# A first row map for two expert slots, and two reorderings in the local attention

## The chip, the cores and the metric

The kernel is written for one Trainium2 chip and runs on one of its cores. A core has five engines with queues of their own: TensorE (PE; its weight loads are shown apart as PEld), VectorE (DVE), ScalarE (ACT), GpSimd (POOL) and SyncE (SP), which here mostly issues DMAs. The metric is the device time of one execution in microseconds (us), the median over several runs. The profile is of one further execution, with a span of its own.

## The reference, cut to what matters

Four blocks work on `x`, four images of 512 tokens with 256 features each (all fp32):

```python
x = x + linear_attention(mixture_of_experts(x, cond))
x = x + local_layers(cond_attention(x, cond))      # two layers

# mixture of experts: 8 experts, each token goes to its two best
gate_w = softmax(rms_norm(x) @ wg_W + wg_b + cond @ gg_W + gg_b)
topk_w, topk_i = top_k(gate_w, 2)
h1 = relu(x @ W1[e] + b1[e]);  h2 = relu(h1 @ W2[e] + b2[e]);  out_e = h2 @ W3[e] + b3[e]
out = sum over the two experts of topk_w * out_e

# each local layer: windowed attention (8 heads of 64, windows of 128), then a gated FFN
q, k, v = split(shift_token(x) @ wqkv)
q, k = rotary_xpos(l2norm(q) * qs, l2norm(k) * ksc)
x = x + softmax(mask(8 * q @ k.T)) @ v @ wo
x = x + (a * gelu(g)) @ w2 + b2                     # a, g from layernorm(shift_token(x)) @ w1 + b1
```

## The kernel before

**Routing and experts.** Tokens are sorted by expert into slots of one or two groups of 128 rows; each slot runs one expert's three matrices. VectorE computes for every token and both of its choices a position, split into a high part (row group and half) and a low part (0 to 63): the tile `hl` (L1438). The *row map* says which token stands in which row. It is made with matmuls: for each of 16 token tiles and both choices, a one-hot of the low part (`ol`, L1456, 64 columns, multiplied by the token number) is the stationary operand and a one-hot of the high part (`oh`, L1461, 80 columns) the moving one; 32 products add up in `pmap`. `half_map` (L1473) copies the sum, two more matmuls fold the halves (`pmap2`), and `rowtok` (L1478) holds the token number of each row, for all 40 row groups, `goal` the row of the output table `ys`. `busy(4)` (L1494) runs four matmuls that no one reads, in program order behind the map.

`loads` (L1508) reads a slot's expert number from `eid` and issues its three weight DMAs on SP's queue (L1511, L1513, L1517); the weight buffers are two deep. `fetch` (L1529) gathers a slot's rows on POOL's queue with `rowtok` as index. `turn_tokens` transposes them on TensorE (`pxb`) and ScalarE copies them out. The loop over the slots runs layer 1 (`ph`), issues the next loads and gathers, the previous slot's last layer (`po`), transposes the next slot's rows, and runs layer 2. Slot 0 has one row group, slot 1 two.

**Order.** Instructions are scheduled by a planner, except those that are pinned: TensorE's in a `PE.in_order()` block, and what goes through `pinned` or `keep_in_program_order`. Each engine then works off its own queue in a fixed order and stops at the first instruction whose inputs are missing.

**Local attention.** `front` (L634) is a generator for one image: two transposed halves (`pdt`), then for four token tiles `t` and for q and k (`s`) a projection `pdq`, its squares on ScalarE (L658), their sums `ss` on VectorE (L659), a product with a table over the whole width (`t1`, L661), two products over half the width (`t2`, L665), and a sum of the two on POOL (L668, `qr`). After all eight: the root on ScalarE (L672), the maximum and reciprocal on VectorE (L673, L674), three value projections, and for each tile the scaling of q (L686) and transposes `pqt` into `qT` and `kT`.

The attention runs in steps `k`, four to an image (`c` is a pair of heads): `scores` (`pds`, exponentials L720, masks L723 and L726), `values` of the step before (`pn`, added into `oT`, L745), and on odd steps `sums`, the denominators of two pairs (`pz`). `sums` goes through DRAM to turn a row into a column and back: `z` to `sums_`, to `rd`, reciprocal (L770), to `rows_` (L772), and two broadcasts into `zb` (L775), all on SP's queue, then two multiplies on `oT` (L778). `beside(b)` is the filler work of the next image's `front` and the previous image's `tail` (`pdy`, the output product that reads `oT`); `spend(n)` takes `n` steps of it. `first_two` (L902) opens each layer with the front of image 0 and two steps of the front of image 1: in layer 0 with nothing beside it, in layer 1 beside the feed-forward work of layer 0.

## Time and profile before

| | us |
|---|---|
| median of 3 runs | 1338.26 (1338.1 to 1339.82) |
| profiled execution, its own time | 1341.16 |
| its span | 1339.4 |
| TensorE busy in it | 1273.7 |
| VectorE busy | 685.6 |
| ScalarE busy | 581.6 |
| POOL busy | 292.8 |

The mean granted clock of TensorE in that execution is 0.983 of full speed. The experts run to about 300 us, the linear and conditioned attention to about 694 us, and the two local layers from there to the end.

Rows of a group or of the timeline read: start or engine, line of the kernel, operation, output tile <- input tiles, partitions x elements, and in brackets how long the engine sat idle before it and what ended that. A matmul in fp32 leaves two records per instruction of the kernel, a transpose one.

### The profile page before, as it was taken

The page shows a single profiled execution, that of the slowest core. Times are in us where ns is not written, and L with a number is a line of the kernel's source. Part 1 is how long each engine was busy: PE and PEld are TensorE (multiplying, and loading weights), DVE is VectorE, ACT ScalarE, POOL GpSimd, SP SyncE. Part 2 cuts the span into 40 slices and gives each one's busy share as a digit, 9 for nine tenths or more (in the row PEclk, how much of TensorE's full clock was granted, in tenths as well). Part 3 has the DMA queues.
Part 4 walks back from the last instruction along what each step waited for, and adds up shares of the span by engine and source line. Part 5 has one row for each costly group of instructions (what it writes and reads, how often), then busy time and mean ns, then how long its engine had stood idle before and what let it go on. Part 6 is the DMA issues. An engine that isn't in the chain of part 4 may idle for free.

```text
span 1339.4 us, 23071 instructions
## 1 busy us (share of the span) xinstructions
PE 1273.7 (95%) x9214; PEld 812.9 (61%) x9214; DVE 685.6 (51%) x1464; ACT 581.6 (43%) x1158; POOL 292.8 (22%) x321
## 2 busy tenths in 40 slices
PE   4899999998999999999999999999999998999998
PEld 3788899964566634444344655766556556667654
DVE  6221243425777734241247798654362877864421
ACT  3221233226655365656644646561222655464111
POOL 1322356420000201010103334210030333422010
PEclk7999999998999999999999999999999999999999
DMA  3565666523000000000220001311001011012000
GB/s 95 212 232 199 233 235 226 183 101 101 0 1 1 1 1 1 0 1 1 91 71 1 18 18 27 104 34 25 24 0 44 25 30 31 18 43 57 17 20 23
DMA packets 41856, 85.29 MB, mean 64 GB/s; under 512 B 9409, under 2 KB 25673, under 8 KB 39433
## 3 DMA queue, kind: packets, MB, share of 16 engines
q1 hardware_dynamic: 36600, 73.02, 16.9%
q0 software_dynamic: 3504, 9.46, 2.1%
q8 instruction: 77, 1.26, 0.4%
q10 hardware_dynamic: 1632, 1.21, 0.3%
q14 instruction: 43, 0.34, 0.1%
HBM read 74.76 MB, written 6.82 MB: 61 GB/s over the span
## 4 chain that ended last, share of the span: by engine, by line
PE 76%; DVE 10%; DMA 6%; ACT 4%; issue 3%; POOL 0%; SPq 0%; DVEq 0%; POOLq 0%
PE ph L82 11%; PE pdq L82 7%; PE pfy L82 6%; PE sc L82 6%; PE pua L82 5%; PE pug L82 5%; PE pv L82 5%; PE pdy L82 4%; PE po L82 3%; PE pn L82 3%; DMA ys<-ob,goal 2%; PE pds L82 2%; PE pqk L82 2%; PE pz L82 1%; PE pqt L86 1%
## 5 line engine op out<-in xcount | busy, mean ns | idle before, releaser
L82 PE MATMUL pdq<-wqkv,yT 128*128 128x512 f32 x384 | 172.4, 599 | 2.5 <-DVE t L665 2.2
L424 ACT ACTIVATE cex<-sc 128x512 f32<-128x512 f32 x256 | 132.0, 605 | 85.8 <-PE sc L82 84.8
L82 PEld LDWEIGHTS pdq<-wqkv,yT 128*128 128x128 f32 x384 | 71.5, 191 | 85.0 <-issue 76.7
L82 PE MATMUL ph<-h,w 128*128 128x256 f32 (+2 forms) x576 | 121.4, 369 | 0.3 <-ACT h L1635 0.3
L668 POOL TENSOR_TENSOR qr<-t,t 128x512 f32<-128x512 f32 x64 | 81.3, 1271 | 138.2 <-DVE t L665 138.2
L82 PEld LDWEIGHTS ph<-h,w 128*128 128x128 f32 x576 | 101.5, 191 | 15.7 <-ACT h L1635 0.5
L1500 DVE TENSOR_SCALAR h<-ph,w 128x256 f32<-128x256 f32 (+2 forms) x52 | 23.0, 462 | 122.1 <-PE ph L82 101.6
L82 PE MATMUL sc<-qm,kT 32*128 32x512 f32 x512 | 83.0, 647 | 0.0
L720 ACT ACTIVATE p<-pds,ss 128x192 f32<-128x192 f32 (+1 forms) x256 | 79.8, 425 | 2.1 <-PE pds L82 0.8
L82 PE MATMUL pua<-hT,w 128*128 128x512 f32 x160 | 75.3, 593 | 1.1 <-DVE z L745 1.1
L82 PE MATMUL pug<-hT,w 128*128 128x512 f32 x160 | 76.1, 598 | 0.0
L658 ACT ACTIVATE sq<-pdq 128x512 f32<-128x512 f32 x64 | 38.5, 601 | 84.0 <-POOL qr L668 46.6
L753 POOL TENSOR_TENSOR p<-p 128x192 f32<-128x192 f32 x64 | 42.1, 678 | 137.7 <-PE pn L82 134.9
L835 ACT ACTIVATE gl<-pug,cols 128x512 f32<-128x512 f32 x40 | 27.3, 687 | 93.3 <-PE pug L82 90.4
L82 PE MATMUL pv<-cex,v 128*32 128x512 f32 x512 | 61.7, 598 | 2.7 <-DVE vw L378 2.7
L82 PE MATMUL pfy<-w,uA 128*128 128x256 f32 x256 | 61.4, 383 | 0.0
L82 PE MATMUL po<-w,h 128*128 128x256 f32 x264 | 60.1, 380 | 0.0
L723 DVE TENSOR_TENSOR p<-p,lmask 128x384 f32<-128x384 f32 x64 | 47.1, 736 | 23.2 <-ACT p L720 21.8
L82 PE MATMUL pdy<-wo,oT 128*128 128x256 f32 x256 | 58.7, 383 | 0.0
L1498 ACT ACTIVATE h<-ph,w 128x256 f32<-128x256 f32 (+2 forms) x52 | 22.4, 455 | 82.5 <-PE ph L82 78.7
L82 PE MATMUL pn<-p,v 64*64 64x128 f32 (+1 forms) x1792 | 50.4, 254 | 7.6 <-DVE p L726 3.7
L836 DVE SCALAR_TENSOR_TENSOR uA<-pua,cols,gl 128x512 f32<-128x512 f32 x32 | 23.8, 749 | 65.6 <-PE pua L82 56.1
(361 smaller groups left out, 2325.1 us busy)
## 6 DMA issues: line engine op xcount, KB each, us to landing
w<-in_moe_w_dram SPq DMA_DIRECT2D x18, 1024.0 KB, 8.3
w<-in_moe_w_dram SPq DMA_DIRECT2D x18, 516.0 KB, 3.8
w<-in_moe_w_dram SPq DMA_DIRECT2D x14, 640.0 KB, 4.3
zb<-rows SPq DMA_DIRECT2D x32, 256.0 KB, 4.2
g<-ys SPq DMA_DIRECT2D x6, 512.0 KB, 6.4
wqkv<-in_f_wqkv_dram SPq DMA_DIRECT2D x2, 1536.0 KB
w<-in_f_w_dram SPq DMA_DIRECT2D x2, 1408.0 KB
w<-in_moe_w_dram SPq DMA_DIRECT2D x4, 512.0 KB
```

Source lines behind the costliest of these rows:

```text
L82: cls._queue(nc.tensor.matmul(*args, **kw))
L86: cls._queue(nc.tensor.transpose(*args, **kw))
L424: nc.scalar.activation(ex[:, i, :], pss[2 * j + i], AF.Exp, scale=CHD**-0.5)
L658: nc.scalar.activation(sq, p3, AF.Square)
L668: nc.gpsimd.tensor_tensor(qr_t[:, s], t1, t2, ALU.add)
L720: nc.scalar.activation(p[:, j * 192 : j * 192 + n], pss[j // 2][r][:, j % 2 * 192 : j % 2 * 192 + n], AF.Exp, scale=d.ss[:, j, 1, 2 * c + ...
L723: nc.vector.tensor_tensor(edges, edges, lmask[:, :128].rearrange("p (s q) -> p s q", q=64).unsqueeze(1).to_broadcast([128, 3, 2, 64]), ALU ...
L753: nc.gpsimd.tensor_tensor(p[:, 1:, 0:64], p[:, 1:, 0:64], p[:, : NT - 1, 128:], ALU.add)
L835: nc.scalar.activation(gl, pg, AF.Gelu, bias=col("bg", l * (NU + 1) + i))
L836: nc.vector.scalar_tensor_tensor(f.u[i // 4][:, i % 4, :], pa, col("ba", l * (NU + 1) + i), gl, ALU.add, ALU.mult)
L1498: pinned(nc.scalar.activation(dst, src, AF.Relu, bias=bias))
L1500: pinned(nc.vector.tensor_scalar(dst, src, bias, 0.0, ALU.add, ALU.max))
```

## The change

*Routing.* Ahead of the full map a first map is made for the three row groups of slots 0 and 1 alone: one-hots of the high part over six columns (`oh0`, which here carries the token numbers), raw one-hots of the low part (`ols`), 32 products of six columns, a copy, two fold matmuls and a `rowtok` of three columns. The gathers of slots 0 and 1 use it. The full map then uses the same `ols`, multiplied by the token numbers in place; three of its four groups of products stand ahead of slot 0's transposes on TensorE, the fourth behind them, and its fold and `rowtok` come after slot 0's first layer. Slot 1's and later weights read the expert number from `eids`, a copy of `eid` that is made behind the full one-hots and depends on the first map. `busy(4)` becomes `busy(7)` ahead of the map, and `busy(2)` and `busy(1)` among the full products. Slot 1's transposes move in between slot 0's second-layer matmuls.

*Local attention.* In `front`, the root, the maximum, the reciprocal and the scaling of the first tile's q move ahead of the last two half products. In layer 0 image 0's first `pqt` bank gets five matmuls of the identity ahead of its transposes. `sums` becomes a generator with two stops: the matmuls, `z` and the first two DMAs come where they were, the reciprocal and the broadcasts at the end of that step, and the multiplies a step later.

```diff
@@ -650,6 +650,11 @@
             d.ss = ss = lp.tile([128, NT, 2, DH], F32, tag="ss", name="ss")
             qr = []
+            def unit(t):
+                tc.keep_in_program_order(nc.vector.tensor_tensor(
+                    qr[t][:, 0], qr[t][:, 0], ss[:, t, 0].unsqueeze(2).to_broadcast([128, DH, DHD]), ALU.mult))
             for t in range(NT):
                 qr_t = lp.tile([128, 2, DH, DHD], F32, tag="qr", name="qr", bufs=4)
                 for s in range(2):
@@ -660,18 +665,22 @@
                     t1 = lp.tile([128, DH, DHD], F32, tag="t1", name="t1")
                     nc.vector.tensor_tensor(
                         t1, p3, w.tab[:, 2 * s, t, :].unsqueeze(1).to_broadcast([128, DH, DHD]), ALU.mult)
+                    if t == NT - 1 and s == 1:
+                        nc.scalar.activation(ss, ss, AF.Sqrt)
+                        tc.keep_in_program_order(nc.vector.tensor_scalar_max(ss, ss, 1e-12))
+                        tc.keep_in_program_order(nc.vector.reciprocal(ss, ss))
+                        unit(0)
                     t2 = lp.tile([128, DH, DHD], F32, tag="tmp", name="t2", bufs=3)
                     for d0, d1 in ((0, 32), (32, 0)):
-                        nc.vector.tensor_tensor(
+                        ins = nc.vector.tensor_tensor(
                             t2[:, :, d0 : d0 + 32], p3[:, :, d1 : d1 + 32],
                             w.tab[:, 2 * s + 1, t, d0 : d0 + 32].unsqueeze(1).to_broadcast([128, DH, 32]), ALU.mult)
+                        if t == NT - 1 and s == 1:
+                            tc.keep_in_program_order(ins)
                     nc.gpsimd.tensor_tensor(qr_t[:, s], t1, t2, ALU.add)
                     yield
                 qr.append(qr_t)
-            nc.scalar.activation(ss, ss, AF.Sqrt)
-            nc.vector.tensor_scalar_max(ss, ss, 1e-12)
-            nc.vector.reciprocal(ss, ss)
             d.v = lp.tile([128, NT, DH, DHD], F32, tag="v", name="v")
             d.kT = lp.tile([128, 4, S], F32, tag="kT", name="kT")
             d.qT = lp.tile([128, 4, S], F32, tag="qT", name="qT")
@@ -683,10 +692,15 @@
                 value(t)
                 yield
             for t in range(NT):
-                nc.vector.tensor_tensor(
-                    qr[t][:, 0], qr[t][:, 0], ss[:, t, 0].unsqueeze(2).to_broadcast([128, DH, DHD]), ALU.mult)
+                if t > 0:
+                    nc.vector.tensor_tensor(
+                        qr[t][:, 0], qr[t][:, 0], ss[:, t, 0].unsqueeze(2).to_broadcast([128, DH, DHD]), ALU.mult)
                 for s, dst in enumerate((d.qT, d.kT)):
                     pt = mmt("pqt")
+                    if t + s == 0 and awake:
+                        with PE.in_order():
+                            for _ in range(awake):
+                                PE.matmul(pt[:, 0:128], ident, ident, start=True, stop=True)
                     for c in range(4):
                         PE.transpose(pt[:, c * 128 : (c + 1) * 128],
                                      qr[t][:, s, 2 * c : 2 * c + 2, :].rearrange("p h d -> p (h d)"), ident)
@@ -763,10 +777,11 @@
                 PE.matmul(later[:, :, 64:], ones32[64:], p[64:, :, 0:64], start=True, stop=True)
                 PE.matmul(later[:, 1:, 0:64], ones32[64:], p[64:, : NT - 1, 64:128], start=True, stop=True)
             together(z, pz)
-            rd = rdenl[:, (l * B + b) * 2 + c // 2, :]
             sums_ = dr.tile([4, S], F32, tag="sums", name="sums")
             nc.sync.dma_start(sums_, z[0:128:32, :])
+            rd = rdenl[:, (l * B + b) * 2 + c // 2, :]
             nc.sync.dma_start(rd, sums_.rearrange("h q -> (h q)").rearrange("(p n) -> p n", p=128))
+            yield
             nc.vector.reciprocal(rd, rd)
             rows_ = dr.tile([4, S], F32, tag="rows", name="rows")
             nc.sync.dma_start(rows_.rearrange("h q -> (h q)").rearrange("(p n) -> p n", p=128), rd)
@@ -774,6 +789,7 @@
             for r in range(2):
                 nc.sync.dma_start(zb[64 * r : 64 * r + 64],
                                   rows_.rearrange("(c r) q -> r c q", r=2)[r].partition_broadcast(64))
+            yield
             for i in range(2):
                 nc.vector.tensor_tensor(d.oT[c - 1 + i], d.oT[c - 1 + i], zb[:, i, :], ALU.mult)
@@ -946,11 +962,13 @@
                     for _ in range(n):
                         next(fill, None)
+                old = iter(())
                 for k in range(4 * B + 2):
                     b, c = divmod(k, 4)
                     if k > 1 and k % 2:
                         b0, c0 = divmod(k - 2, 4)
-                        sums(l, b0, ds[b0], c0)
+                        young = sums(l, b0, ds[b0], c0)
+                        next(young)
                     if c == 0 and b < B:
                         run(fill)
                         fill = beside(b)
@@ -959,7 +977,13 @@
                         values(ds[b0], c0)
                     if b < B:
                         scores(ds[b], c)
+                    if k % 2 == 0:
+                        run(old)
                     spend(6 if b < B - 1 else 3)
+                    if k > 1 and k % 2:
+                        old = young
+                        next(old)
+                run(old)
                 spend(2)
                 for _ in tail(wa, B - 1, ds[B - 1]):
                     next(ff)
...
@@ -1360,6 +1384,14 @@
             pcnt = mmt("pcnt")
             PE.matmul(pcnt[:, :NE], tot, mtiles[:, 128:], start=True, stop=True)
             PE.matmul(ppos[:, :128], tot, mtiles[:, :128], start=False, stop=True)
+            def busy(n):
+                with PE.in_order():
+                    ps = mmt("pbusy")
+                    for _ in range(n):
+                        PE.matmul(ps, ident, xres[0].rearrange("p t h -> p (t h)")[:, :512], start=True, stop=True)
+            busy(7)
             E2 = [128, NE, 3 * NE]
             over = xp.tile(E2, F32, tag="over", name="over")
             nc.vector.tensor_tensor(over, pcnt[:, :NE].unsqueeze(2).to_broadcast(E2),
@@ -1448,50 +1481,98 @@
+            def one_hot(out, of, iota):
+                shape = list(of.shape) + [iota.shape[1]]
+                for _ in of.shape[1:]:
+                    iota = iota.unsqueeze(1)
+                tc.keep_in_program_order(nc.vector.tensor_tensor(
+                    out, of.unsqueeze(len(of.shape)).to_broadcast(shape), iota.to_broadcast(shape), ALU.is_equal))
+            first = [2 * NPAIR + SLOTS[0][0], 2 * SLOTS[1][0], 2 * SLOTS[1][0] + 1]
+            oh0 = y[2].rearrange("p t h -> p (t h)")[:, : 12 * B * NT].rearrange("p (k i n) -> p k i n", k=2, n=6)
+            for at, r, n in ((0, first[0], 2), (2, first[1], 4)):
+                one_hot(oh0[:, :, :, at : at + n], hl[:, 0], miota[:, 2 * r : 2 * r + n])
+            tokens = mtok.rearrange("p (k i) -> p k i", k=2)
+            pinned(nc.vector.tensor_tensor(
+                oh0, oh0, tokens.unsqueeze(3).to_broadcast([128, 2, B * NT, 6]), ALU.mult))
+            ols = [y[k].rearrange("p t h -> p (t h)").rearrange("p (i n) -> p i n", n=64) for k in (1, 3)]
+            for i0 in (0, B * NT // 2):
+                for k in range(2):
+                    one_hot(ols[k][:, i0 : i0 + B * NT // 2], hl[:, 1, k, i0 : i0 + B * NT // 2], miota[:, :64])
+            def map_products(pmap, n, onehot, k, tiles):
+                for i in tiles:
+                    PE.matmul(pmap[64 * k : 64 * k + 64, : 2 * n], ols[k][:, i, :], onehot(k, i),
+                              start=(i == 0), stop=(i == B * NT - 1))
+            def map_copied(pmap, n):
+                half_map = xp.tile([128, n, 2], F32, tag=f"hmap{n}", name="hmap")
+                pinned(nc.vector.tensor_copy(half_map, pmap[:, : 2 * n].rearrange("p (r q) -> p r q", q=2)))
+                return half_map
+            def map_rows(half_map, n):
+                pmap2 = acct("pmap2")
+                for q in range(2):
+                    PE.matmul(pmap2[64 * q : 64 * q + 64, :n], mfold, half_map[:, :, q], start=True, stop=True)
+                rowtok = xp.tile([128, n], I32, tag=f"rowtok{n}", name="rowtok")
+                pinned(nc.vector.tensor_scalar(rowtok, pmap2[:, :n], -1.0, 0.0, ALU.add, ALU.max))
+                pinned(nc.vector.tensor_single_scalar(rowtok, rowtok, B * S - 1, op=ALU.bitwise_and))
+                return pmap2, rowtok
...
+            with PE.in_order():
+                pmap = acct("pmap")
+                for i in range(B * NT):
+                    for k in range(2):
+                        map_products(pmap, 3, lambda k, i: oh0[:, k, i, :], k, [i])
+                early_rows = map_rows(map_copied(pmap, 3), 3)[1]
+            xbs = [hp.tile([128, 2, H], F32, tag="xb", name="xb", bufs=3) for j in range(2)]
+            gather(xbs[0][:, 0, :], early_rows, 0)
+            for i in range(2):
+                gather(xbs[1][:, i, :], early_rows, 1 + i)
+            eids = xp.tile([128, 1], I32, tag="eids", name="eids")
             pmap = acct("pmap")
...
+            ohs = []
+            def full_onehots(g):
+                tiles = slice(4 * g, 4 * g + 4)
+                oh = hp.tile([128, 2, 4, NHI], F32, tag=f"h{1 + g // 2}", name="oh")
+                one_hot(oh, hl[:, 0, :, tiles], miota)
+                for i in range(4 * g, 4 * g + 4):
+                    pinned(nc.scalar.mul(ols[0][:, i, :], ols[0][:, i, :], mtok[:, i : i + 1]))
+                pinned(nc.vector.tensor_tensor(
+                    ols[1][:, tiles], ols[1][:, tiles], tokens[:, 1, tiles].unsqueeze(2).to_broadcast([128, 4, 64]),
+                    ALU.mult))
+                ohs.append(oh)
+            def full_products(g):
                 with PE.in_order():
+                    for i in range(4 * g, 4 * g + 4):
+                        for k in range(2):
+                            map_products(pmap, NROWT, lambda k, i: ohs[i // 4][:, k, i % 4, :], k, [i])
+            for g in range(4):
+                full_onehots(g)
+            pinned(nc.vector.scalar_tensor_tensor(eids, early_rows[:, 0:1], 0.0, eid, ALU.min, ALU.max))
+            busy(2)
+            for g in range(3):
+                full_products(g)
+                if g == 0:
+                    busy(1)
+            def full_rows():
+                pmap2, rowtok = map_rows(full_map, NROWT)
...
+                return rowtok, goal
...
-                e = nc.sync.value_load(eid[j : j + 1, 0:1], min_val=0, max_val=NE - 1)
+                e = nc.sync.value_load((eids if j else eid)[j : j + 1, 0:1], min_val=0, max_val=NE - 1)
...
@@ -1571,6 +1650,8 @@
                         m = m2 * k + i
                         mm(ps[:, i * n : (i + 1) * n],
                            [(w[:, c, m * 128 : (m + 1) * 128], src[:, c, 0:n]) for c in range(w.shape[1])])
+                        if between is not None and m == 2:
+                            between()
                     if d.n == 2:
                         turn[0] ^= 1
                     for i in range(k):
@@ -1707,10 +1788,12 @@
             btail = y[3][:, 0]
             htail = y[2].rearrange("p t h -> p (t h)")[:, 512:].rearrange("p (w c n) -> p w c n", w=NWIDE, c=4)
             loads(0, ds[0])
-            fetch(0, ds[0])
-            fetch(1, ds[1])
+            ds[0].xb, ds[1].xb = xbs
             with PE.in_order():
                 turn_tokens(ds[0])
+                full_products(3)
+            with PE.in_order():
+                full_map = map_copied(pmap, NROWT)
             last_wide = max(j for j, d in enumerate(ds) if d.wide)
             often, rare = ds[:-NRARE], range(len(ds) - NRARE, len(ds))
             for j, d in enumerate(often):
@@ -1728,6 +1811,8 @@
                         h1 = layer_few(d, d.xbT, d.t1, "h1", w1, d.s1, 0)
                     else:
                         h1 = layer(d, d.xbT, "h1", w1, 0)
+                    if j == 0:
+                        rowtok, goal = full_rows()
                     if j + 1 < len(often):
                         loads(j + 1, after)
                         for name in list(later)[: (j > 1) + (j > 8)]:
...
@@ -1756,9 +1839,9 @@
                     if 9 < j < 10 + B:
                         pinned(nc.gpsimd.tensor_tensor(
                             xres[j - 10], xres[j - 10], row("bo").unsqueeze(1).to_broadcast([128, NT, H]), ALU.add))
-                    if j + 1 < len(often):
+                    if 0 < j < len(often) - 1:
                         turn_tokens(after)
-                    d.h2 = layer(d, h1, "h2", d.w2, 4)
+                    d.h2 = layer(d, h1, "h2", d.w2, 4, None if j else lambda: turn_tokens(after))
                     if d.wide:
                         pinned(nc.scalar.copy(htail[:, d.at], d.h2[:, :, 256:]))
             last(len(often) - 1, often[-1])
```

Not shown: `first_two` passes the number of filler matmuls to `front` (five in layer 0, none in layer 1), and `gather` replaces the written-out gathers of the other slots.

## The prediction

> **What bounds the kernel now.** I read the busy shares first, then the chain of work that ended last in the two places that the diff touches, then the waits of TensorE and the DMAs behind them. TensorE bounds the whole:
>
> ```profile
> PE 1273.7 (95%) x9214; PEld 812.9 (61%) x9214; DVE 685.6 (51%) x1464; ACT 581.6 (43%) x1158; POOL 292.8 (22%) x321
> ```
>
> So only a stretch in which TensorE waits, or runs at a low clock, can give time back. The first is the routing. The chain there (start, length, what):
>
> ```profile
> 30.27 0.21 DVE hl L1438
> 30.50 0.69 DVE ol L1456
> ...
> 37.10 1.02 PE pmap L82 x16
> ...
> 39.51 5.26 DMA xb<-in_x_dram,rowtok
> 44.82 0.45 PE pxb L86 x2
> ...
> 45.71 3.58 PE ph L82 x16
> 49.29 0.44 PE pxb L86 x4
> 49.75 7.80 PE ph L82 x48
> ```
>
> From `hl` at 30.5 the map of all 40 row groups is built, the first gather leaves at 39.51 and takes 5.26, and the first expert starts at 45.71. From there to 257 us the chain is TensorE almost without a break, so what is won before 45.71 stays won. The busy time by stretch, whose columns after the five engines are granted clock, DMA share and GB/s:
>
> ```profile
> 30.00:35.00 5.00, 2.82 (x32) 2.64 (x32) 4.93 (x11) 2.55 (x10) 0.00 (x0) 0.50 0.83 281
> 35.00:40.00 5.00, 3.90 (x43) 2.55 (x41) 3.07 (x10) 1.70 (x7) 0.49 (x1) 0.97 1.01 415
> 40.00:45.00 5.00, 2.57 (x8) 0.95 (x6) 0.00 (x0) 0.00 (x0) 3.78 (x5) 1.00 0.74 282
> 45.00:50.00 5.00, 4.52 (x24) 4.04 (x23) 0.27 (x1) 0.74 (x2) 1.53 (x2) 0.66 0.27 79
> ```
>
> Two things: the gather competes with the weights of slots 0 and 1 (DMA share 1.01), and the clock falls to half as the first expert starts (0.66 over that stretch), so its 16 records take 3.58 us.
>
> The second place is the local attention. TensorE's waits in layer 0 (total, times, longest):
>
> ```profile
> PE pqt L86 <- DVE qr L686: 5.8, 4, 2.5
> PE pn L82 <- DVE p L723: 1.8, 2, 0.9
> ```
>
> And VectorE's reciprocal and broadcast multiply, which stand in its queue:
>
> ```profile
> 785.65 0.24 DVE L770 RECIPROCAL rden<-rden 128x16 f32<-128x16 f32 x1
> ...
> 792.55 1.28 DVE L778 TENSOR_TENSOR oT<-oT,zb 128x512 f32<-128x512 f32 x2
> ```
>
> Here the multiply did not wait, and TensorE's `pdy`, which reads `oT`, began at 795.36.
>
> **The change, part by part: routing.** VectorE after `hl` first makes the one-hots of six columns (64, 128, then a product of 192 elements; by the 128x128 row of 0.20 and the 128x192 row of 0.36 about 0.7) and four compares of 512 elements at 0.60 spacing (2.4): the first pair is done at 32.4, the last at 33.6. TensorE then runs 32 products, 64 records. The last `pmap` group shows 55 ns per load and 63 per matmul, the first group, at half clock, 85. I take 60: 3.8 us, so 32.5 to 36.3; 33.6 plus the second half at 55 ns, 35.4, is the early end, 37.9 with 85 ns the late one. Copy, fold, two small operations and the issue took 1.39 (38.12 to 39.51); with 3 columns for 40 I take 1.2. The gather leaves at 37.5 for 39.51.
>
> The Trainium skill (TensorE: Matmul & The Clock Gate, Back-to-back issue gap) gives matmuls of up to 64 columns an issue floor of about 25 ns. By it the 64 records would be 1.6 us and the gather would leave about 0.9 us earlier, bounded by the compares; the row's 55 ns is a load that such a matmul can't hide, and I keep it.
>
> Slot 1's weights now wait for `eids`, the last of VectorE's full one-hot work: four times 0.74 and 0.34 from 37.2, so 41.6, and SP issues about 1.0 later as it did after `eid`. So the gather meets a free DMA: 2.9 us as `xtail`, or 3.5 as the median gather, landed by 41.0. TensorE isn't ready then. Its queue holds two busy matmuls (4 records of 0.43), three groups of full products (1.0 each, by the 1.01 row) and one more busy matmul (0.86), 5.6 us from 36.85: the transposes come at 42.4. After 0.45 of these stands the fourth group, 1.0, and the expert starts at 43.85 instead of 45.71: 1.85 won. TensorE has then not idled, so I take the clock as full: 16 records at 0.12 are 1.9 for 3.58, 1.65 won. Four transposes that filled a gap now stand among the second layer's matmuls: 0.4 lost. Sum 3.1; the ends are 0 (cold products 1.6 later, cold expert) and 4.5 (no busy filler in the way).
>
> Costed at nothing: slot 1's first weights, issued at 42.6 and landing 3.8 later, are wanted near 51; its second, 8.3 after issue, at 51.5, wanted at 54.5. The full map's VectorE work lies beside TensorE's 8 us of slot 0, and the gathers of slot 2 on POOL move from 43.4 to about 47, wanted at 59. SP's other loads are queued behind the late pair, but wait for slot 0's buffers (55.8 before) anyway.
>
> **Local attention: reciprocal ahead.** In the built order the maximum, reciprocal and first scaling now stand ahead of the last two half products (0.66) for each front. At 748 they were also slowed by POOL (1.18 for one scaling that takes 0.6 alone); POOL's sum now comes later. The first `pqt` of image 1 moves from 750.09 to 748.8: 1.2 won, again in layer 1. In the opening front ScalarE's root ends at 715.14 as before; only the POOL slowdown goes (0.4), the second scaling moves behind a copy (`qr` 1 at about 718.6), but the five filler matmuls leave TensorE idle for about 1 us rather than 2.52, and the clock, which fell at 718.0 and made 16 transposes take 2.92 and 4 projections 2.42 (1.75 and 1.72 at full clock), should hold: 1.0 won, between 0.5 lost and 1.9.
>
> The Trainium skill (TensorE: Matmul & The Clock Gate, What's actually happening) says that the clock drops after at least one idle window of about 3.4 us. By it neither gap would have cooled and both clock gains (1.65 and 1.0) would be nil; here it fell after 2.5 us idle, so a mostly idle window is enough.
>
> **Local attention: broadcasts later.** From reciprocal to the end of the wait for `zb` six cases give 6.93, 6.83, 7.82, 6.52, 6.40, 6.47: 6.8, with 6.4 and 7.8 as ends. Image 1: the reciprocal no longer blocks the masks (0.5 won at 764), runs at 763.0, and VectorE is free at 771.1 for 772.2: 1.0 won in all. Image 2: the reciprocal moves from 785.65 to behind the last whole product, 789.15, so 788.15 with that gain. Then `zb` lands at 794.95, one multiply takes 0.6, and the third `pdy` step, at 796.25 before, comes at 795.55: TensorE now stands there for nearly 2 us, and of the 2.3 won at `pqt` only 0.7 is left. Image 3, reckoned in the same way: 844.45 for 845.4, 0.95. At the last broadcast (858.23 before, behind which TensorE lost 1.1) the reciprocal follows two masks: 0.45 lost. Layer 0: 0.5. Layer 1 by the same steps: 0.8 left of image 1, 0.4 after image 2, 1.1 after image 3, 0.4 lost: 0.7.
>
> Sum: 3.1 + 1.0 + 0.5 + 0.7 = 5.3. The profiled execution took 1341.16 (span 1339.4 and 1.8 around it), which would become 1335.9; it stands 2.9 above the median of the runs shown, 1338.26, and to that the same sum gives 1333.0.
>
> **Rivals.** (1) The routing wins little: the small products or the first expert run at half clock, or slot 1's weights come last. For it: 0.50 granted from 18.5 to 35.2, and a load moved by 10 us with 3 us in hand. Against it: seven busy matmuls ahead of the products, twelve records that keep TensorE at work. Gain 0 to 1.5 instead of 3.1: 1334.6 to 1336.1, and with a cold opening front too (1.5 more) 1337.6.
> (2) The late broadcasts decide, and the kernel is slower: `pdy` in two images and the last broadcast, in each layer, are six places where TensorE waits for `zb`. Each us by which it lands later than 6.8 costs 6 us. From 7.7 on everything won is gone; 1.5 later, 8.3, gives 1342. One case of 7.8 and a chain with 8.34 for the DMA alone speak for it, the five cases under 7.0 against.
> (3) More is won: the gather is in time, the fillers don't bind, and image 2's `zb` lands in 6.4: 1.4 and 6 x 0.4 more, 1329.2.
>
> **How the numbers follow.** Forecast (1330.5 to 1335.5) 0.52, rival 1 0.20, rival 2 0.10, rival 3 0.16, others 0.02. The range 1328.5 to 1338.2 leaves out most of rival 2 and the end of rival 3. 0.2%, about what a measurement of this kernel tells from no change, is 2.7 us: faster is below 1335.6, which takes the forecast, rival 3 and a little of rival 1, 0.71; the same 0.20; slower 0.09.
>
> **What would show it.** Right: the first gather issued near 37.5 and landing in about 3 us; `ph` from about 43.9 in under 2.1 us at clock 1.0; slot 1 without a wait for `w`; `pqt` of image 1 without a wait for `qr`; a new wait of `pdy` for `oT` of 1 to 2 us. Wrong: `pmap` over 80 ns per record, a clock of 0.5 at the expert or at the opening `pqt`, TensorE waiting for `w`, or `pdy` waits above 3 us.

## The result, and the profile after

The change made the kernel slower: 1343.96 us (median of 22 runs) against 1338.09 for the kernel before (22 runs), a ratio of 1.0044 (95% interval 1.0031 to 1.0056), 5.9 us. The forecast was 1333.0, and its range, up to 1338.2, did not hold the time. The profiled execution after took 1344.84, its span is 1343.1. The start times of a few marked pieces of work show where its lead grew and where it went:

| start of, us | before | after | after less before |
|---|---|---|---|
| first gather's issue | 39.51 | 37.02 | -2.49 |
| first expert's `ph` | 45.71 | 44.22 | -1.49 |
| last result scatter's issue | 293.32 | 290.77 | -2.55 |
| copies of the results | 297.44 | 296.61 | -0.83 |
| local layers, first `pdt` | 694.23 | 691.47 | -2.76 |
| layer 0, first `pdq` behind image 0 | 719.89 | 718.35 | -1.54 |
| layer 1, first `pdt` | 959.90 | 964.25 | +4.35 |
| TensorE's last instruction (end) | 1333.71 | 1337.65 | +3.94 |

So the routing's lead came about and reached the local layers; layer 0 lost 7 us of it. TensorE's busy time in the page of after is 9.6 us up on before:

```profile
PE 1283.3 (96%) x9304; PEld 813.2 (61%) x9304; DVE 686.1 (51%) x1471; ACT 581.4 (43%) x1158; POOL 296.4 (22%) x321
```

The chain of work that ended last, at the routing (start, length, what):

```profile
30.29 0.21 DVE hl L1470
...
33.81 1.89 PE pmap L82 x30
...
36.32 3.71 PE pbusy L82 x4
40.04 0.86 PE pmap L82 x16
...
44.29 2.00 PE ph L82 x16
...
46.73 3.45 PE ph L82 x24
50.17 0.44 PE pxb L86 x4
```

The first expert's 16 records now take 2.00 instead of 3.58 (the chain counts them from the end of the group ahead, 44.29). But four `pbusy` records ahead of it take 3.71, 0.93 each, twice what they need at full clock. The busy time by stretch says why (clock, DMA share and GB/s at the end of a row): from 35 to 40 the granted clock is half, while TensorE counts as busy.

```profile
30.00:35.00 5.00, 3.86 (x59) 2.64 (x60) 3.65 (x10) 2.41 (x10) 0.00 (x0) 0.85 0.81 273
35.00:40.00 5.00, 4.74 (x22) 2.10 (x20) 3.76 (x10) 1.63 (x7) 2.40 (x2) 0.50 0.53 203
40.00:45.00 5.00, 5.00 (x76) 3.80 (x76) 1.32 (x4) 0.37 (x1) 1.48 (x1) 0.97 0.61 170
45.00:50.00 5.00, 4.79 (x40) 4.27 (x39) 1.29 (x6) 0.73 (x2) 1.26 (x2) 1.00 0.81 330
```

TensorE's waits in both local layers (total, times, longest). Before, `pdy` waited for nothing and `pqt` for `qr` 9.5 us in 7 places:

```profile
PE pqt L86 <- DVE qr L686: 9.5, 7, 2.5
...
PE pds L82 <- DVE t L665: 2.2, 3, 1.0
```

After:

```profile
PE pdy L82 <- DVE oT L794: 6.5, 5, 2.3
PE pds L82 <- DVE t L675: 4.9, 5, 1.4
...
PE pqt L86 <- DVE qr L696: 2.0, 1, 2.0
```

And VectorE's timeline at the sums of image 1 in layer 0 (L785 is the reciprocal, L794 the multiply by `zb`):

```profile
761.43 0.24 DVE L785 RECIPROCAL rden<-rden 128x16 f32<-128x16 f32 x1
769.79 1.29 DVE L794 TENSOR_TENSOR oT<-oT,zb 128x512 f32<-128x512 f32 x2 [3.05 <-DMA zb<-rows]
788.13 0.23 DVE L785 RECIPROCAL rden<-rden 128x16 f32<-128x16 f32 x1
795.64 1.29 DVE L794 TENSOR_TENSOR oT<-oT,zb 128x512 f32<-128x512 f32 x2 [1.43 <-DMA zb<-rows]
```

From reciprocal to landed `zb` it is 8.36 and 7.51 here, where 6.8 was taken. In the first case VectorE stands for 3.05 with the next image's half products behind the multiply: hence the 4.9 of `pds` for `t`, 2.2 before.

### The profile page after: what moved, and what is told of

It is laid out like the page before. It is cut to its first block, busy times and chain, and to the rows that moved or that the text cites. A ratio compares the mean times of both kernels' runs of the same rounds, so it can differ in the third digit from the quotient of the medians.

```text
span 1343.1 us, 23273 instructions
## 1 busy us (share of the span) xinstructions
PE 1283.3 (96%) x9304; PEld 813.2 (61%) x9304; DVE 686.1 (51%) x1471; ACT 581.4 (43%) x1158; POOL 296.4 (22%) x321
## 4 chain that ended last, share of the span: by engine, by line
PE 69%; DVE 11%; DMA 9%; ACT 5%; issue 3%; POOL 1%; SPq 1%; DVEq 0%; POOLq 0%
PE ph L82 11%; PE sc L82 6%; PE pfy L82 5%; PE pua L82 5%; PE pv L82 5%; PE pug L82 5%; PE pdq L82 4%; PE pdy L82 3%; PE po L82 3%; DMA zb<-rows 3%; DMA ys<-ob,goal 2%; PE pn L82 2%; DVE t L666 1%; PE pqk L82 1%; DMA rows<-rden 1%
## 5 line engine op out<-in xcount | busy, mean ns | idle before, releaser
L680 POOL TENSOR_TENSOR qr<-t,t 128x512 f32<-128x512 f32 x64 | 84.0, 1312 | 154.9 <-DVE t L675 154.9
L82 PEld LDWEIGHTS pdy<-wo,oT 128*128 128x128 f32 x256 | 47.0, 190 | 20.6 <-DVE oT L794 10.3
L1579 ACT ACTIVATE h<-ph,w 128x256 f32<-128x256 f32 (+2 forms) x52 | 22.4, 455 | 78.4 <-PE ph L82 74.5
```

The source lines that it names most:

```text
L82: cls._queue(nc.tensor.matmul(*args, **kw))
L680: nc.gpsimd.tensor_tensor(qr_t[:, s], t1, t2, ALU.add)
L1579: pinned(nc.scalar.activation(dst, src, AF.Relu, bias=bias))
```

## The experiments

All ratios are to the kernel before, run on the same chip beside it; the times are medians.

### The three parts alone, and the change without the broadcasts

Theory 1 was that the later broadcasts cost the time, theory 2 that the norms' new place in VectorE's order does; beside it stood the question of whether the routing's lead lasts. `routing_only` is the changed kernel with the hunks of `front`, `first_two`, `sums` and the step loop taken back, `norms_only` and `sums_only` are the kernel before with one set of hunks each. `no_sums` is the changed kernel with this:

```diff
-            yield
             nc.vector.reciprocal(rd, rd)
...
-            yield
             for i in range(2):
                 nc.vector.tensor_tensor(d.oT[c - 1 + i], d.oT[c - 1 + i], zb[:, i, :], ALU.mult)
...
-                        young = sums(l, b0, ds[b0], c0)
-                        next(young)
+                        sums(l, b0, ds[b0], c0)
```

> The kernel before with the routing part of the change alone. Theory 1 (the profiled lead of 2.55 us at 256 us is kept, and what was lost of it around the results' transfers in one profile, 2.0 us, is chance): the last expert scatter is issued at 290.8 (293.3 before), the first product of linear attention begins near 303.3 (305.84 before), the time is 1335.5, ratio 0.9980. Theory 2 (the results' transfers take the lead back, whatever comes before them): the first product of linear attention begins at 305.2 to 305.9 again, time 1337.5 to 1338.2, ratio 0.9995 or more.

> The changed kernel with the sums' broadcasts put back to where they were before; routing and norms stay as changed. Theory 1 (the broadcasts cost the time): the waits of the output products pdy for the multiply by zb (6.5 us in the profile after) are gone, and with them the late half products on VectorE; the stage from 694 us on, 5.8 us longer in the profile after (lead 2.75 at 694, lag 3.7 at the end: 6.5), gets shorter than before's by 2 to 5 us; time 1331 to 1334, ratio 0.995 to 0.997. Theory 2 (the norms' new place in VectorE's order costs it): the stage from 694 us on stays 3 us or more longer than before's, time 1338 to 1342, ratio 1.000 or more.

> The kernel before with the later broadcasts alone. Theory 1: pdy waits for the multiply by zb again, 5 us or more in all, and the time is 1345 to 1349, ratio 1.005 to 1.008. Theory 2: pdy waits for little (under 2 us), time 1337.5 to 1339, ratio 1.000 within 0.001. A theory between (the two edits collide only where both are made): pdy waits are under 3 us and the time 1338 to 1341.

> The kernel before with the norms' reciprocal ahead and the five records ahead of the first transposition alone. Theory 1: 1.0 to 1.1 us won at the first transposed queries of each image but the first of layer 0, where 1.2 us is lost as in the profile after (first products of image 1 at 2.75 us ahead turned into 1.54 ahead): 6 or 7 times 1.05 less 1.2 is 5 to 6 us, so 1332 to 1334, ratio 0.995 to 0.9965. Theory 2: what is won at the transpositions is lost later through VectorE's changed order; time 1338 to 1342, ratio 1.000 or more.

| | us | ratio (95%) |
|---|---|---|
| `routing_only` | 1340.61 | 1.0015 (0.9997 to 1.0032) |
| `no_sums` | 1335.56 | 0.9983 (0.9965 to 1.0001) |
| `sums_only` | 1347.01 | 1.0071 (1.0043 to 1.0099) |
| `norms_only` | 1334.86 | 0.9974 (0.9960 to 0.9988) |

Theory 1 holds in direction: with the broadcasts alone the kernel is 9 us slower, without them the change is no slower than before, and the norms win 3.4 us. But `no_sums` and `norms_only` both stay short of what theory 1 gave them (1331 to 1334, 1332 to 1334), for reasons that the later sections find. TensorE's waits in `sums_only`, and then in `norms_only`, where `pqt` waits 3.4 us instead of 9.5:

```profile
PE pdy L82 <- DVE oT L780: 7.4, 4, 4.1
```

```profile
PE pqt L86 <- DVE qr L696: 2.0, 1, 2.0
...
PE pqt L86 <- DVE qr L655: 1.4, 3, 0.5
```

The 9 us of `sums_only` are more than the broadcasts alone. 4.1 of its 7.4 stand at one place, where SyncE's queue has the load of a table (`tab`, 128 packets of 4 KB) just ahead of `rows`:

```profile
837.65 0.34 SPq L199 DMA_DIRECT2D tab<-in_rot_dram  x1
838.04 0.42 SPq L773 DMA_DIRECT2D rows<-rden  x1
841.58 1.25 SPq L776 DMA_DIRECT2D zb<-rows  x2
```

The packets of `rows` start 2.24 us after its issue there, at most 0.85 in all other cases, and `zb` lands 9.77 after the reciprocal. In before and after this load stands behind `zb`.

The routing fitted neither expectation for it. In its profile the local layers were reached at 689.28, 4.95 ahead of before, and yet the time was no better: these layers took 644.1 us instead of 639.5, though all engines have the same instructions in the same order there. With the norms it was the same (637.3 with the routing, 632.9 without).

### What of the broadcasts costs: the chain or the multiply

`early_chain` keeps only the multiplies late, `late_chain` keeps the reciprocal and the transfers late and puts the multiplies right behind them:

```diff
-            yield
             nc.vector.reciprocal(rd, rd)
...
                         old = young
-                        next(old)
```

```diff
-            yield
             for i in range(2):
...
-                        old = young
-                        next(old)
+                        run(young)
```

> The changed kernel with the sums' reciprocal and both broadcast transfers issued at their old place, right behind the sums; only the multiplication by the broadcast sums keeps its later place. Theory 1 (the chain from the reciprocal to the landed broadcast takes 6.4 us or more, and starting it up to 2.9 us later is what pdy waits for): the transfer of the reciprocal's result is issued 1.8 to 2.5 us after that of the sums' return again (2.7 to 5.2 us in the profile after), pdy waits for the multiplication under 1 us in all, and the time is that of the kernel with old broadcasts, 1334 to 1337. Theory 2 (the place of the multiplication, behind the next values' sum in VectorE's order, is what pdy waits for): pdy still waits 4 us or more, time 1341 to 1345.

> The changed kernel with the reciprocal and the broadcast transfers at their new, later place, and the multiplication right behind them in the program instead of a step later. Theory 1 (the late chain): pdy still waits for the multiplication, 5 us or more in all, one time near 1344. Theory 2 (the late multiplication): pdy waits under 2 us, one time near 1337.

`early_chain`: 1335.59, ratio 0.9978 (0.9963 to 0.9993), the time of the kernel with old broadcasts. Its page has `pdy` (instructions, busy, mean ns, idle before):

```profile
L82 PE MATMUL pdy<-wo,oT 128*128 128x256 f32 x256 | 59.3, 384 | 0.1
```

`late_chain`, one execution: 1343.01, and TensorE's waits have:

```profile
PE pdy L82 <- DVE oT L793: 5.9, 4, 2.1
```

So the late start of the reciprocal and its transfers is the cost; the later multiply costs nothing that these runs show.

### The opening of layer 0

In all profiles with the old opening and a full clock, 24.7 us pass from the stage's first `pdt` to the first `pdq` behind image 0; with the changed one 26.05 at a full clock (one profile) and 26.8 to 26.9 where the clock fell. `norms_later_images` leaves the first image of layer 0 as before; `norms_no_records` keeps its new order and drops the five records. Both are shown against `norms_only`, cut:

```diff
-                    if t == NT - 1 and s == 1:
+                    if ahead and t == NT - 1 and s == 1:
...
+            if not ahead:
+                nc.scalar.activation(ss, ss, AF.Sqrt)
+                nc.vector.tensor_scalar_max(ss, ss, 1e-12)
+                nc.vector.reciprocal(ss, ss)
...
-        lead, second = first_two(wa, ds, 5)
+        lead, second = first_two(wa, ds, False)
```

```diff
-        lead, second = first_two(wa, ds, 5)
+        lead, second = first_two(wa, ds, 0)
```

> The kernel before with the norms' reciprocal ahead in every image but the first of layer 0, whose opening stays as before, without the five records. Theory 1 (the opening as changed costs 1.3 us: from its first transposition of the stage to image 1's first product 24.72 us where the opening is unchanged and the clock full, 26.05 us with the changed one): this stretch takes 24.7 us at a full clock (25.7 if the clock falls in it), the time is 1333.5, 1.3 below the kernel with all of the norms' change (1334.9). Theory 2 (the changed opening wins 1.0 us, as forecast): the time is 1335.9. A rival of both: within 0.3 of 1334.9.

> The kernel before with the norms' reciprocal ahead in all images, without the five records ahead of the first transposition (with them 1334.9; with the first image as before 1331.5). If the records cost it: the stretch from the stage's first transposition to image 1's first product takes 24.8 to 25.2 us at full clock instead of 26.05, time 1331.5 to 1332.5. If VectorE's order costs it (the second scaling behind two half products and a copy): 25.7 us or more, time 1334 to 1335.

`norms_later_images`: 1331.54, ratio 0.9953 (0.9936 to 0.9970); its opening takes 24.73. `norms_no_records`: 1334.13, ratio 0.9987 (0.9973 to 1.0000); 26.88, with a clock of 0.53 from 717 to 720. So it is the order that costs; the records do no harm that shows (0.9974 with them). VectorE's timeline of `norms_no_records` shows it:

```profile
713.16 0.20 DVE L670 TENSOR_SCALAR ss<-ss 128x64 f32<-128x64 f32 x1 [1.50 <-ACT ss L669]
713.38 0.55 DVE L671 RECIPROCAL ss<-ss 128x64 f32<-128x64 f32 x1
713.97 0.69 DVE L655 TENSOR_TENSOR qr<-qr,ss 128x512 f32<-128x512 f32 x1
714.58 0.75 DVE L675 TENSOR_TENSOR t<-pdq,tab 128x256 f32<-128x256 f32 x2
715.48 0.69 DVE L707 COPY qT<-pqt 128x512 f32<-128x512 f32 x1
716.08 2.34 DVE L696 TENSOR_TENSOR qr<-qr,ss 128x512 f32<-128x512 f32 x3
```

VectorE stands for 1.50 on ScalarE's root with the half products queued behind it; before, they ran in that time. They and a copy (`qT`) now come between the first and the second scaling: the first tile is ready 0.4 us sooner after the stage's first `pdt` (22.4 for 22.8), the second 1.6 later (25.0 for 23.4). The five records don't shorten TensorE's standing either: in `norms_only` it is 0.52 and 1.99, in before 2.52 in one. In the later images `pqt` waits little (0.9 in all in `norms_later_images`).

The half clock is part of the price: it falls at the opening in seven of the eight profiles with the changed order and in two of the eight with the old one, where it adds 0.4 to 0.9 us.

### Why the routing's lead is lost: the place of the code

The one thing that the routing alone changes in the local layers is which buffers four tiles get. `routing_same_buffers` gives them the old ones, by four one-column writes at the start:

```diff
     y = [resp.tile([128, NT, H], F32, tag="res", name=f"ymoe{b}") for b in range(B)]
+    for b in (0, 2, 1, 3):
+        tc.keep_in_program_order(nc.gpsimd.memset(y[b][:, 0, 0:1], 0.0))
```

> The kernel with the routing part alone, and four one-column writes on GpSimd at the start that give the expert results and the local attention's residual tiles the buffers that they have in the kernel before (the routing change alone exchanges them); the order of all other engines is that of routing_only. Theory A (the exchanged buffers make the shifted copies hn land late: first one used 4.1 to 4.9 us after its issue in three profiles without the routing change, 5.7 to 6.4 us in three with it, and the local stage 2.7 to 4.7 us longer): first hn used after 4.1 to 4.9 us, stage from 694 us on as long as before's, time 1335.5. Theory B (it is where in time these transfers fall, or chance): hn and the time as in routing_only, 5.7 us or more and 1339 to 1341. Theory C (the routing's lead is worth its 2.5 us and the first 12 runs were unlucky): hn as it falls, time 1335 to 1337.

It took 1342.14, ratio 1.0015 (0.9996 to 1.0034), and the first `hn`, a copy of half of `yc` shifted by one token, was used 6.78 us after its issue. Theory A falls. That copy is on the chain that ended last, in before and in after:

```profile
803.70 2.34 DMA hn<-yc
```

```profile
804.11 3.81 DMA hn<-yc
```

The trace has a further traffic. Part 3 of every page lists a queue q8 of kind "instruction" with 77 or 78 packets of 16 KB. TensorE's 18,428 records in before make 239 to a packet, and the packets go by the count of these records: from the 21st on, a packet starts at the same count in before and in after (median difference 0, four in five within 72). The routing adds 160 records, the whole change 180 (x9304 for x9214, twice), and so moves all later packets, against the work, by two thirds to three quarters of their distance. For the first `hn` copy:

| kernel | code packet starts after `hn`'s issue | `hn` first used after |
|---|---|---|
| before, `sums_only` | 5.95, 5.57 | 4.90, 4.88 |
| `norms_only`, `norms_later_images` | 4.26, 4.84 | 4.07, 4.13 |
| after, `routing_only` | 3.16, 3.14 | 6.38, 6.43 |
| `no_sums`, `early_chain`, `late_chain` | 2.75, 4.16, 3.19 | 5.71, 6.44, 6.10 |

Undisturbed, `hn`'s last packet ends 4.49 after the issue (before) or 3.63 (`norms_only`, which issues its parts closer together): a code packet ahead of that makes it late. The same shows at `rows`, the 8 KB transfer behind the reciprocal. SyncE's timeline of after, then the DMA traffic from the issue to 763.2, with a packet of q8 among it, and from there to the next issue:

```profile
761.70 0.33 SPq L787 DMA_DIRECT2D rows<-rden  x1
764.98 1.33 SPq L790 DMA_DIRECT2D zb<-rows  x2
```

```profile
q1 hardware_dynamic: 135, 0.01, 5.8%
q8 instruction: 1, 0.02, 3.6%
```

```profile
q1 hardware_dynamic: 9, 0.00, 0.9%
```

Here 3.28 us pass for 1.55 without it, and that makes the 8.36 of the chain above, 6.80 without it (in `after_padded`, below). Nine of the 144 packets, one sixteenth, start only from 763.64 on, when the code packet (762.78 to 763.66) ends. In the sixteen profiles, 256 such transfers, 241 took 1.40 to 1.57 us and fifteen 1.84 to 3.54. Fourteen of the fifteen have a code packet in them (nine of q8, five with packets of 8 KB of the other such queue, q14), and in each the last packet of the transfer starts 0.04 to 0.08 us after the code packet's end; the fifteenth is the one behind `tab`. In the first `hn` of `routing_same_buffers` 479 of 511 packets start by 4.48, and the other 32, again a sixteenth, from 4.89, with the code packet from 3.17 to 4.91.

If so, the place of the code alone must cost time, and moving it back must win it. `code_shift` is the kernel before with 160 records of tiny products in idle stretches of TensorE ahead of 32 us; in the padded kernels the records added become 256, by an estimate from the count above about one packet, and their pages list 78 packets of q8 instead of 77:

```diff
             ptot = mmt("ptot")
-            PE.matmul(ptot[:, 0:1], flat, ones, start=True, stop=True)
+            with PE.in_order():
+                for _ in range(24):
+                    PE.matmul(ptot[0:1, 0:1], ident[0:1, 0:1], ident[0:1, 0:1], start=True, stop=True)
+                PE.matmul(ptot[:, 0:1], flat, ones, start=True, stop=True)
...
             pmap = acct("pmap")
+            with PE.in_order():
+                for _ in range(16):
+                    PE.matmul(pmap[0:1, 0:1], ident[0:1, 0:1], ident[0:1, 0:1], start=True, stop=True)
```

`routing_padded` and `best` have the first half of this, 24 products, `after_padded` and `no_sums_padded` 19. `best` is the routing with the norms of `norms_later_images` and old broadcasts.

> The kernel before with 40 one-column products (160 records) in two idle stretches of TensorE ahead of 32 us, and nothing else changed: its code stands where the routing change puts it. Theory F: the packet of code falls into the first hn copy, which is used 5.7 us or more after its issue, the stage from 694 us on takes 642 to 644 us and the time is 1341 to 1343 (1338.2 before), slower although no work is added on the path. Theory B: hn 4.1 to 4.9 us, time 1338.

> The routing part alone, plus 24 one-column products (96 records of weight load and product) in TensorE's idle stretch ahead of 21.5 us, so that together with the routing's own 160 its instruction stream grows by 256 records' worth of code, one 16 KB packet of the trace's instruction queue q8. Theory F (with the routing change a 16 KB packet of instruction code falls into the first shifted copy hn, 2.75 to 4.2 us after its issue in six profiles, and holds one of 16 DMA engines for 1.0 to 1.7 us; without it the packet comes 4.3 to 5.9 us after, when the copy has landed): the packet falls behind the copy again, hn is used 4.0 to 4.9 us after its issue, the stage from 694 us on takes 637 to 640 us (644.1 and 642.3 with the routing change), time 1335.5. Theory B (the code's place does not matter): hn 5.7 us or more, stage 642 or more, time 1340 to 1342.

> The changed kernel with 19 one-column products, which make its 180 added records 256. Theory F: first hn after 4.9 us or less; the later broadcasts still cost their 4 to 5 us, so 1340 to 1341 instead of 1344. Theory B: 1344.

> The changed kernel with old broadcasts and with its code put back to where before had it by 19 one-column products; beside the padded changed kernel, 1338.0, it tells the price of the later broadcasts alone. If they cost what pdy waits for in that kernel's profile (4.2 us) and 1 to 2 us of late half products: 1332 to 1333. If most of the 8.4 us came from collisions with the code packets: 1335.5 or more, under 2.5 us for the broadcasts. If they cost as much at any place of the code: 1329.5.

> Routing, the norms' reciprocal ahead in all images but the first of layer 0, old broadcasts, and 24 one-column products that put the code back to where before had it. Theory F: the 2.5 us of the routing come on top of the norms' gain, 1329 (the norms alone in these images: 1331.5). Theory B: the routing wins nothing here either, or costs 1 to 4 us, 1331.5 to 1335.5.

| | us | ratio (95%) | without the padding | first `hn` used after |
|---|---|---|---|---|
| `code_shift` | 1343.86 | 1.0036 (1.0021 to 1.0051) | 1 (before) | 6.64 |
| `routing_padded` | 1336.22 | 0.9988 (0.9973 to 1.0002) | 1.0015 | 4.90 |
| `after_padded` | 1337.98 | 0.9991 (0.9975 to 1.0008) | 1.0044 | 4.89 |
| `no_sums_padded` | 1330.26 | 0.9948 (0.9933 to 0.9963) | 0.9983 | 4.04 |
| `best` | 1329.99 | 0.9932 (0.9916 to 0.9948) | not run | 4.06 |

Theory F holds in four pairs: 160 records that do nothing make the kernel before 4.8 us slower (of which its profile shows 1.0 at the first expert's start, where the records themselves are late), and a few more records of nothing make the changed kernel 7.1 us faster (0.0053 of 1338). Not every size came as expected. `code_shift`'s local layers took 640.9 in its profile, 1.4 more than before, for an expected 642 to 644 (layer 0 took 3.6 more, layer 1 2.2 less), and `after_padded` is 2 us under its 1340. SyncE's timeline of `after_padded` at the same place, where no code packet falls:

```profile
762.59 0.33 SPq L787 DMA_DIRECT2D rows<-rden  x1
764.14 1.33 SPq L790 DMA_DIRECT2D zb<-rows  x2
```

Its TensorE waits still have the price of the later broadcasts:

```profile
PE pdy L82 <- DVE oT L794: 4.2, 4, 1.6
...
PE pds L82 <- DVE t L675: 1.9, 2, 1.0
```

Beside `no_sums_padded` (0.9948) they cost 0.0043, 5.8 us, at this place of the code; a difference of two ratios is uncertain by about 3 us. Beside `no_sums` it was 0.0061. The two waits of TensorE shown here, 6.1 in sum, were 11.4 in after: 5.3 us less. The time of `no_sums_padded` lies between its first expectation and its third and does not tell them apart. `best`, which leaves them out and the old opening in, beats both kernels; the waits of `best`:

```profile
PE pqt L86 <- DVE qr L700: 2.5, 1, 2.5
PE pdq L82 <- DVE t L675: 2.4, 4, 0.7
```

## Why the prediction was wrong, point by point

**"So only a stretch in which TensorE waits, or runs at a low clock, can give time back."** The sum had no term for the work that the change adds off the path. 180 records, costed by their duration alone, moved TensorE's code packets onto short transfers that the local layers wait for: about 7 us, more than the whole gain that was forecast. No rival had it, and it is not among the terms that were "costed at nothing". This is the largest term, and the one that turned the sign: with the code moved back the changed kernel is at 0.9991, no slower than before, though 1.2 us won is still far from 5.3. A sign of it was in the profile of before: the 7.82 that gave the upper end for `zb` and spoke for rival 2 has a code packet in its transfer, 4.89 us after the reciprocal.

**"What is won before 45.71 stays won."** Right as to the path: 2.55 us of lead at the last scatter, 2.76 at the local layers. Part of it was lost between these in the profile (2.55 to 0.83) and won back by the clock: it was up again 1.8 earlier at 310, and before's profile alone has half the clock from 632.6 to 636.0. In after a code packet started 1.67 us after the last scatter's issue, and the scatter's last packet ended at 3.67; before, the code packet started at 2.11, as the scatter ended. At that edge it falls either way: among 16 profiles the copies were issued 4.1 to 4.3 us after the scatter in seven and 5.4 to 6.2 in nine, with the routing and without.

**Routing, 3.1 won.** 2.55 in the profile; with the code in its old place the routing alone measured 1.6 (0.9988, interval from 3.6 won to 0.3 lost). The first gather left at 37.02 for a forecast 37.5, the 62 records of the map took 50 ns each for 60, `ph` 2.00 for 1.9, slot 1 did not wait for weights: right. The step that failed is "TensorE has then not idled, so I take the clock as full". The clock fell during the small products or right behind them for 3.4 or 6.8 us in every profile with the routing, and `ph` started at 42.9 to 43.5 in the four where it fell for 3.4 and at 44.2 to 45.0 in the six where it was 6.8 (forecast 43.85).

The Trainium skill (TensorE: Matmul & The Clock Gate, What's actually happening) has a free-running window of 3413 ns, and the stretches of 3.4 and 6.8 us agree with that; its rule that the clock falls after an idle window would have kept it up here, where 62 records fill 3.08 us, and the measurement decides against it. By its issue floor (Back-to-back issue gap, some 25 ns) the 64 records would have been 1.6 us; they took 2.30 for 62 in `routing_only`, all at full clock, 37 ns each. The sentence that draws on it also has a slip: with the compares done at 33.6 and half of the records at 25 ns behind them the products end at 34.4 for 36.3, so the gather would leave 1.9 us earlier and not 0.9.

**Opening front, 1.0 won.** Wrong in sign: about 1.3 lost at a full clock by the trace (one profile, `norms_only`), 2.8 by the two ratios (0.9974 and 0.9953, a difference uncertain by about 3 us). The step weighed the POOL slowdown and the clock, and noted that the second scaling moves behind a copy, but it did not charge VectorE's 1.50 of standing on the root with the half products behind it: the second tile was to be ready at about 718.6, 24.4 after the stage's first `pdt`, and was at 25.0. The records were to leave TensorE idle for about 1 us and left 2.5, and they don't keep the clock up reliably either: half the clock for 3.4 us somewhere between 715 and 721 in six of seven profiles with them. Nor does "a mostly idle window is enough" hold by itself: the old opening stands for 2.5 us in all eight profiles with it, and the clock fell in two.

**Reciprocal ahead, 1.2 at image 1's `pqt`.** Right, and in all six later images: `pqt`'s waits for `qr`, 7.0 there before (9.5 less the opening's 2.5), are 0.9 in `norms_later_images`, which won 6.3.

**Broadcasts later.** The mechanism was right: at the old place of the code, from reciprocal to landed `zb` the kernel needed 6.80, 6.88, 6.43 and 6.71 in the first four cases where 6.8 was taken, and `pdy` waited up to 1.6 where "1 to 2 us" stood. Together with the norms they were to win 1.2; 6.3 won and 5.8 lost make 0.5. So the later broadcasts give nearly all of the norms' gain back, which was the forecast, with the size off by 0.7, less than these runs can tell (about 3 us). In the changed kernel itself `zb` was later (8.36, 7.51, 7.85, 7.25), as in rival 2, and the time was near its 1342. But the chain is not longer than 6.8 by itself: a code packet lay in each of the four. Not each one harms: `after_padded`'s 6.88 has one too.

The terms at hand, 6.3 won by the norms, 2.8 lost at the opening, 5.8 lost by the broadcasts, 1.6 won by the routing and 7.1 lost by the code's place, add up to 7.8 lost; 5.9 was measured. A term read from one ratio is uncertain by about 2 us, one read from two by about 3, so that the sum agrees but proves no single term.

## What to carry to other kernels

Reading a result a step later was free here, starting the chain of transfers that produces it a step later is not: of a chain that goes through DRAM move only its consumer. An instruction that waits, put ahead of ready work on an in-order queue, must be charged with the work behind it, and the same reordering can win beside other work and lose where nothing stands beside it. When a kernel that only adds work off the path turns out slower in a part that it doesn't touch, compare the places of the code packets in both traces before explaining anything else, and try a few empty instructions.

## What the runs showed of the hardware that was not expected

TensorE's code arrives by the same DMA engines as the data, in packets of 16 KB that take 0.9 to 2.0 us. One that falls into a transfer of a few KB delays the whole of it: `rows` from 1.40 to 1.57 us to between 1.8 and 3.5, the first `hn` copy by 1.2 us or more. The instruction count ahead of a stage decides where they fall, so 160 empty records were worth 0.36% of the time. What waits is one sixteenth of the transfer's packets, as if one of the 16 engines were held up; the trace doesn't name a packet's engine. It leaves a part open too: in after's first `rows` the last packet comes 1.0 us later than in `after_padded`, the next issue 1.7.

The clock fell to half under a TensorE that its records show as busy: in all ten profiles with the first map, after 64 records of six columns (3.08 us for 62 of them in after), for 3.4 or 6.8 us. It also falls for 3.4 us around a standing of about 2.5 us at the opening of the local layers, in two of eight profiles with the old order and in seven of eight with the changed one, so that neither a gain nor a loss there can be read from one profile.
